# Transposing tokens on VectorE in 32x32 blocks instead of on TensorE, in a transformer block with routed experts

## The chip, the cores and the metric

The kernel runs on one core of a Trainium2 chip. The metric is the device time in microseconds, the median of several runs. All data is float32.

A core has five engines that each run their own list of instructions in order: TensorE (PE, matmuls; PEld is its loading of weights), VectorE (DVE), ScalarE (ACT), GpSimd (POOL) and SyncE (SP), which only issues transfers. Transfers run on 16 DMA engines. An engine that waits for a semaphore holds up everything behind it in its list.

## The reference

The input is x with 32 batches of 256 tokens of 128 features, 8192 tokens in all. Shift, scale and gate vectors for each batch come from a small product (`mod`). Then:

```python
h = _layernorm(x) * (1 + ca) + sa
x = x + ga * attn(h)        # 16 heads of 64; RMS norm of h first; softmax over the query axis
h = _layernorm(x) * (1 + cb) + sb
x = x + gb * moe(h)         # 32 experts in 4 groups: 2 groups a token, 6 experts among them,
                            # one anchor of 16, and a shared expert
```

What matters here is that products over features need the features of `h` on the partitions, while norms and rows in memory have a token on each partition. So each set of tokens is transposed, [tokens, features] to [features, tokens], at three places: ahead of attention, ahead of routing, and once more for each tile of tokens of the experts.

## The kernel before, in words

**Attention.** The tokens are cut into 16 chunks of 512 (`CH`), each as four blocks of 128 (`NT`). A step `s` is one pair of heads of one chunk, so there are 128 steps, eight for each chunk. The order is written out by hand (`manual_schedule`): a loop over `s` issues score products (`psc`, L438), the reduction of each row (`lowest`, L458, VectorE), exponentials (L468, ScalarE), the products with the values (`pav`, L505), query, key and value products of later steps (`pq` L402, `pk` L414, `pv` L388) and the projection (`po`, L526). Everything else that a chunk needs stands in `table`: a portion of work, the step relative to the chunk's first step, and the place in that step (TOP, MID or END). For instance

```python
(-8, END, norm1_scale),
(-5, END, norm1_turn),
...
(17, END, norm2_turn),
(18, END, route_logits),
```

mean that chunk c's first norm is finished at step 8c - 8 and turned at the end of step 8c - 5. `norm1_turn` and `norm2_turn` call `transposed`: four TensorE transposes (L326) into one PSUM bank, then a copy by ScalarE (L378, L571). `norm1_turn` makes `n_t`, the operand of the query, key and value products; `norm2_turn` makes `h2_all[c]`, the operand of `route_logits` and of the shared expert.

SP issues the transfers of this half: `load_x` and `load_mod1` at step -15 of a chunk, `load_mods` at step 7, and the 69 blanks. A blank writes 512 empty rows to `rows_d`, a buffer in device memory that takes the tokens sorted by expert group. A row there has 180 floats (720 bytes): the 128 features of a token, then 52 floats of routing weights and its place. GpSimd scatters each chunk's rows into it (`route_send`, L768).

**Shared expert and expert tiles.** After the steps a loop of seven rounds does the shared expert (`shared_up`, `shared_down`) beside the last portions of `table`. Then come 35 tiles (`LISTS`) of 512 rows of one group. Tile j has five rounds k (four pairs of experts and the anchors): `up` makes `pg` and `pu` (L1141, L1142), ScalarE the silu, VectorE two products (L1145 with `pu`, L1146 with the routing weights `bt`), and `down` sums into `py` (L1167). Work for later tiles is mixed in: `fetch_rows(j + 3)` and `fetch_weights(j + 2)` at k = 0, `weights_mine(j + 2)` at k = 1, `weights_turn(j + 2)` at k = 2, `rows_turn(j + 1)` at k = 3. `weights_turn` transposes the routing weights (L1109), writes them to device memory (`cd`, L1113) and, when that has landed, reads them back once for all partitions (`bt`, L1116, L1121). `rows_turn` transposes the rows' features by four TensorE transposes (L1132) and a copy by ScalarE (L1134).

`send(j)` scatters a tile's result to `y_d` (L1178). When all tiles of a chunk are surely done, `pass_load` (two loads `s`, L1234, and a gate, L1239) at k = 4, `pass_sum` at k = 1 of the next tile and `pass_out` (L1256) at k = 3 finish the chunk. With the levels of this kernel there is one `pass_load` in each of tiles 17 to 27, then in 29, 30, 33 and 34. All these transfers are issued by SP in program order.

## Time and profile before

| | us |
|---|---|
| median of 3 runs | 1537.22 (1533.1 to 1537.77) |
| profiled execution, its own time | 1516.82 |
| span of that execution, first to last instruction | 1515.0 |
| busy: TensorE, VectorE, ScalarE, GpSimd | 1447.8, 1019.8, 837.3, 775.2 |
| mean granted TensorE clock | 0.987 |
| first score product, first expert tile | 39.6, 986.3 |

Four transposes and one copy turn one chunk or tile. In the profile by forms they are:

| line | what | instructions | mean ns |
|---|---|---|---|
| L326 | `ptn`, TensorE | 64 | 299 |
| L326 | `pth`, TensorE | 64 | 289 |
| L1132 | `ph`, TensorE | 140 | 273 |
| L378, L571, L1134 | copies, ScalarE | 16, 16, 35 | 585 |

How to read it: matmuls overlap in TensorE's pipeline, so a mean of 273 to 299 ns is not what one of them adds to the time; the distance between the starts of what stands before and after is. The share of busy time says little where halves of the program have different limits, so the slices, the windows and the chain of waits are read by stage.

### The profile page before, as it was taken

The page shows a single profiled execution, that of the slowest core. Times are in us where ns is not written, and L with a number is a line of the kernel's source. Part 1 is how long each engine was busy: PE and PEld are TensorE (multiplying, and loading weights), DVE is VectorE, ACT ScalarE, POOL GpSimd, SP SyncE. Part 2 cuts the span into 40 slices and gives each one's busy share as a digit, 9 for nine tenths or more (in the row PEclk, how much of TensorE's full clock was granted, in tenths as well). Part 3 has the DMA queues.
Part 4 walks back from the last instruction along what each step waited for, and adds up shares of the span by engine and source line. Part 5 has one row for each costly group of instructions (what it writes and reads, how often), then busy time and mean ns, then how long its engine had stood idle before and what let it go on. Part 6 is the DMA issues. An engine that isn't in the chain of part 4 may idle for free. (4 is left out here: it accounts for less than half of the span.)

```text
span 1515.0 us, 29937 instructions
## 1 busy us (share of the span) xinstructions
PE 1447.8 (96%) x8784; PEld 920.3 (61%) x8784; DVE 1019.8 (67%) x4239; ACT 837.3 (55%) x2796; POOL 775.2 (51%) x1311
## 2 busy tenths in 40 slices
PE   3999999999999999999999999899999999999994
PEld 1566666666666666666666666566666666565662
DVE  2655677677677677787677676666755556666663
ACT  1877677677677677676776767433333333333331
POOL 5335457567566566576576554744322324333333
PEclk7999999999999999999999999999999999999997
DMA  6970001000100100100110000576676677888862
GB/s 226 379 267 23 8 28 37 28 27 29 41 30 27 41 29 28 39 32 27 39 32 25 23 23 28 145 201 185 185 182 188 188 195 229 244 227 236 221 179 67
DMA packets 100073, 166.27 MB, mean 110 GB/s; under 512 B 15365, under 2 KB 58853, under 8 KB 95433
## 3 DMA queue, kind: packets, MB, share of 16 engines
q1 hardware_dynamic: 87096, 141.47, 32.8%
q0 software_dynamic: 10624, 20.21, 3.8%
q10 hardware_dynamic: 2192, 2.68, 0.5%
q8 instruction: 73, 1.20, 0.3%
q14 instruction: 88, 0.71, 0.2%
HBM read 113.51 MB, written 51.58 MB: 109 GB/s over the span
## 5 line engine op out<-in xcount | busy, mean ns | idle before, releaser
L468 ACT ACTIVATE e<-e,mn 128x256 f32<-128x256 f32 (+1 forms) x1024 | 454.6, 445 | 211.0 <-DVE mn L458 210.3
L458 DVE CUSTOM_DVE_ANT_0 e<-psc,mask 128x256 f32<-128x256 f32 (+1 forms) x1024 | 306.1, 346 | 63.5 <-PE psc L438 62.4
L1178 POOL DMA_INDIRECT y_d<-y,iy x140 | 139.6, 997 | 301.0 <-ACT y L1175 268.7
L487 POOL TENSOR_TENSOR vs<-v,rc 128x256 f32<-128x256 f32 x256 | 151.2, 611 | 272.5 <-DVE rc L476 249.2
L1145 DVE TENSOR_TENSOR a<-a,pu 128x512 f32<-128x512 f32 x175 | 119.9, 685 | 158.8 <-PE pu L1142 158.6
L438 PE MATMUL psc<-q,k 64*128 64x256 f32 (+1 forms) x2048 | 202.1, 337 | 0.0
L505 PE MATMUL pav<-e,vs 128*64 128x256 f32 (+1 forms) x2048 | 195.3, 333 | 4.2 <-POOL vs L487 4.2
L1144 ACT ACTIVATE a<-pg 128x512 f32<-128x512 f32 x175 | 104.5, 597 | 170.0 <-PE pg L1141 167.7
L1167 PEld LDWEIGHTS py<-wd_sb,a 128*128 128x128 f32 x1120 | 145.6, 192 | 84.1 <-issue 43.9
L407 DVE TENSOR_SCALAR q<-pq,negbq 128x512 f32<-128x512 f32 x128 | 96.0, 750 | 148.1 <-PE pq L402 147.6
L468 ACT ACTIVATION_READ_ACCUMULATOR e<-e,mn 128x1 f32 x1024 | 191.6, 187 | 0.0
L438 PEld LDWEIGHTS psc<-q,k 64*128 64x128 f32 x2048 | 166.4, 187 | 28.2 <-issue 7.9
L1141 PE MATMUL pg<-h,wg 128*128 128x512 f32 x350 | 179.7, 595 | 0.0
L1142 PE MATMUL pu<-h,wu 128*128 128x512 f32 x350 | 178.8, 593 | 0.0
L526 PEld LDWEIGHTS po<-wo_sb,z 128*128 128x128 f32 x1024 | 134.9, 193 | 59.6 <-issue 59.6
L505 PEld LDWEIGHTS pav<-e,vs 128*64 128x64 f32 x2048 | 127.1, 137 | 56.7 <-POOL vs L487 4.5
L1167 PE MATMUL py<-wd_sb,a 128*128 x1120 | 149.4, 277 | 11.3 <-DVE a L1146 11.1
L768 POOL DMA_INDIRECT rows_d<-rows,ix x128 | 130.7, 1021 | 37.2 <-issue 34.2
L388 PE MATMUL pv<-wqkv_sb,n_t 128*128 128x512 f32 x256 | 145.4, 652 | 4.0 <-DVE q L407 3.2
L402 PE MATMUL pq<-n_t,wqkv_sb 128*128 128x512 f32 x256 | 144.1, 645 | 0.0
L526 PE MATMUL po<-wo_sb,z 128*128 128x128 f32 x1024 | 136.3, 277 | 0.0
L414 PE MATMUL pk<-n_t,wqkv_sb 128*128 128x512 f32 x256 | 130.8, 592 | 0.0
(214 smaller groups left out, 1851.2 us busy)
## 6 DMA issues: line engine op xcount, KB each, us to landing
bt<-cd SPq DMA_DIRECT2D x70, 512.0 KB
rows_d<-blank SPq DMA_DIRECT2D x69, 360.0 KB
rw<-rows_d SPq DMA_DIRECT2D x35, 360.0 KB
wg<-in_w_gate_dram SPq DMA_DIRECT2D x35, 256.0 KB
wu<-in_w_up_dram SPq DMA_DIRECT2D x35, 256.0 KB
bt<-cd SPq DMA_DIRECT2D x140, 64.0 KB
mb<-mod_dram SPq DMA_DIRECT2D x32, 256.0 KB
s<-y_d SPq DMA_DIRECT2D x32, 256.0 KB
```

The costliest lines, as they stand in the source:

```text
L388: nc.tensor.matmul(pv, chunk[c]["n"][:, i * P : (i + 1) * P], wqkv_sb[:, 2, j * CH : (j + 1) * CH], start=True, stop=True,)
L402: nc.tensor.matmul(pq, wqkv_sb[:, 0, t * P : (t + 1) * P], chunk[c]["n"], start=True, stop=True)
L438: nc.tensor.matmul(pb[h][:, cols], k[r, o + kb * P : o + (kb + 1) * P], q[r, o + kb * P : o + S], start=True, stop=True,)
L458: nc.vector.tensor_tensor_reduce(e[:, cols], ps[:, cols], mask[:, cols], 1.0, 3e38, ALU.add, ALU.min, mn[:, b, kb, h : h + 1],)
L468: nc.scalar.activation(e[:, cols], e[:, cols], AF.Exp, bias=mn[:, b, kb, h : h + 1], scale=-1.0, accum_out=sm[:, b, kb, h : h + 1],)
L487: nc.gpsimd.tensor_tensor(vs[:, 2 * b : 2 * b + 2], vt[:, 2 * b : 2 * b + 2, col : col + P].rearrange("p k (h d) -> p k h d", h=2), rc[:, ...
L505: nc.tensor.matmul(pav[h * DH : (h + 1) * DH, o + kb * P : o + S], vs[:, 2 * b + kb, h, :], e[:, 0 : 2 * P] if kb == 0 else e[:, 2 * P : 3 ...
L526: nc.tensor.matmul(chunk[c]["po"][:, i, :], z[:, i * P : (i + 1) * P], wo_sb[:, t, :], start=t == 0 and i == 0, stop=t == NP - 1 and i == ...
L1141: nc.tensor.matmul(pg, t["wg"][:, k, :], t["h"], start=True, stop=True)
L1142: nc.tensor.matmul(pu, t["wu"][:, k, :], t["h"], start=True, stop=True)
L1167: nc.tensor.matmul(t["py"][:, i, :], a[:, i * P : (i + 1) * P], w, start=k == 0 and i == 0, stop=k == KU and i == NT - 1,)
L1178: sent = nc.gpsimd.indirect_dma_start(out=y_d[:, :], out_offset=bass.IndirectOffsetOnAxis(ap=ix[:, i : i + 1], axis=0), in_=y[:, i, :], in ...
```

## The change

Three turns go from TensorE and ScalarE to VectorE, whose transpose works inside 32x32 blocks. So the blocks must be in place before: `load_blocks` reads the tokens from device memory with four transfers, one for each 32 features, that put piece c of every 32 tokens on partition 32b + c. In memory such a piece is 32 floats, 128 bytes, and a set of 512 tokens has 2048 of them.

- `norm1_turn` (but for chunk 0) and `norm2_turn`: a new portion, `norm1_send` at -7 END and `norm2_send` at 16 END, writes the tokens to a buffer in device memory (`hd`, two buffers) and reads them back by blocks (`through_dram`); the turn is one VectorE transpose. `norm1_turn` moves from -5 END to -5 MID, `norm2_turn` from 17 END to 19 TOP, `route_logits` from 18 to 19 END. The buffer `hb` has the tag of the normalized tokens (`xhln1`, `xhln2`), so it takes their place.
- Tiles: `fetch_rows` loads the 52 floats of routing (208 bytes a row) and the features apart, by four block loads; `rows_turn` is one VectorE transpose. The order of a tile's tokens goes from `(p i)` to `(i p)`.
- Blanks: three a step, after the portions at END, instead of five a step ahead of everything.

```diff
+        hdp = actx.enter_context(tc.tile_pool(name="hd", bufs=2, space=DRAM))
...
+        def load_blocks(dst, rows):
+            return [
+                nc.sync.dma_start(
+                    out=dst[b * BLK : (b + 1) * BLK],
+                    in_=rows[:, b * BLK : (b + 1) * BLK].rearrange("(x c) r -> c x r", c=BLK),
+                )
+                for b in range(P // BLK)
+            ]
+
+        def through_dram(src, tag, name):
+            hd = hdp.tile([CH, D], F32, tag="hd", name=f"hd_{name}")
+            nc.sync.dma_start(out=hd.rearrange("(i p) d -> p i d", p=P), in_=src)
+            hb = ln.tile([P, CH // BLK, BLK], F32, tag=tag, name=f"hb_{name}")
+            load_blocks(hb, hd)
+            return hb.rearrange("p x r -> p (x r)")
...
         def norm1_turn(c):
-            nc.scalar.copy(n_t, transposed(chunk[c].pop("h"), f"ptn_{c}"))
+            if c == 0:
+                nc.scalar.copy(n_t, transposed(chunk[c].pop("h"), f"ptn_{c}"))
+            else:
+                nc.vector.transpose(n_t, chunk[c].pop("hb"))
+        def norm1_send(c):
+            if c > 0:
+                chunk[c]["hb"] = through_dram(chunk[c].pop("h"), "xhln1", f"ln1_{c}")
...
         def norm2_turn(c):
-            nc.scalar.copy(h2_all[c], transposed(chunk[c]["rows"][:, :, 0:D], f"pth_{c}"))
+            nc.vector.transpose(h2_all[c], chunk[c].pop("hb2"))
+        def norm2_send(c):
+            chunk[c]["hb2"] = through_dram(chunk[c]["rows"][:, :, 0:D], "xhln2", f"ln2_{c}")
...
-            (-5, END, norm1_turn),
+            (-7, END, norm1_send),
+            (-5, MID, norm1_turn),
...
-            (17, END, norm2_turn),
-            (18, END, route_logits),
+            (16, END, norm2_send),
+            (19, TOP, norm2_turn),
+            (19, END, route_logits),
...
-            for i in blanks[s * 5 : s * 5 + 5]:
-                write_blank(i)
...
             deal(s, END)
+            for i in blanks[s * 3 : s * 3 + 3]:
+                write_blank(i)
...
-            t["rw"] = rwp.tile([P, NT, ROW], F32, tag="rw", name=f"rw_{j}")
-            got = nc.sync.dma_start(
-                out=t["rw"],
-                in_=rows_d[bass.ds(r, CH), :].rearrange("(p i) f -> p i f", i=NT),
-            )
+            t["rw"] = rwp.tile([P, NT, ROW - D], F32, tag="rw", name=f"rw_{j}")
+            t["rh"] = rwp.tile([P, CH // BLK, BLK], F32, tag="rh", name=f"rh_{j}")
+            rows = rows_d[bass.ds(r, CH), :]
+            got = [
+                nc.sync.dma_start(
+                    out=t["rw"], in_=rows[:, D:].rearrange("(i p) f -> p i f", p=P)
+                ),
+                *load_blocks(t["rh"], rows),
+            ]
...
         def rows_turn(j):
             t = T[j]
-            rw = t.pop("rw")
-            ph = ps_mm.tile([P, CH], F32, tag="mm", name=f"ph_{j}")
-            for i in range(NT):
-                nc.tensor.transpose(ph[:, i * P : (i + 1) * P], rw[:, i, 0:D], ident)
             t["h"] = mp.tile([P, CH], F32, tag="h", name=f"h_{j}", bufs=2)
-            nc.scalar.copy(t["h"], ph)
+            nc.vector.transpose(t["h"], t.pop("rh").rearrange("p x r -> p (x r)"))
```

More of the change, by code (lines that the diff above doesn't have):

```diff
@@ L28 @@
 BPC = CH // S
+BLK = 32
 NCH = B * S // CH
@@ L1063, in fetch_rows @@
             r = nc.sync.value_load(of.table[0:1, 1, n : n + 1], min_val=0, max_val=NG * SPAN)
-            t["rw"] = rwp.tile([P, NT, ROW], F32, tag="rw", name=f"rw_{j}")
-            got = nc.sync.dma_start(
-                out=t["rw"],
-                in_=rows_d[bass.ds(r, CH), :].rearrange("(p i) f -> p i f", i=NT),
-            )
-            if j < FIRST:
-                tc.declare_no_dep(
-                    got.ins, group="late rows", reason="this tile holds rows of earlier chunks"
-                )
-                tc.add_to_no_dep_group("first tiles", got.ins)
+            t["rw"] = rwp.tile([P, NT, ROW - D], F32, tag="rw", name=f"rw_{j}")
[7 more added lines that the diff above has]
+            ]
+            if j < FIRST:
+                for d in got:
+                    tc.declare_no_dep(
+                        d.ins, group="late rows", reason="this tile holds rows of earlier chunks"
+                    )
+                    tc.add_to_no_dep_group("first tiles", d.ins)
         def fetch_weights(j):
@@ L1093, in weights_mine @@
                 mm,
-                t["rw"][:, :, D:].rearrange("p i (g w) -> p i g w", w=GW),
+                t.pop("rw").rearrange("p i (g w) -> p i g w", w=GW),
                 of.mine[:, n, :].unsqueeze(1).unsqueeze(3).to_broadcast([P, NT, NG, GW]),
```

## The prediction

> **What bounds the kernel now.** I read the slices first. TensorE is full from start to end; the 16 DMA engines are nearly idle in the attention half and 50 to 80% busy in the expert half.

> ```profile
> PE   3999999999999999999999999899999999999994
> ...
> DMA  6970001000100100100110000576676677888862
> ```

> A full row could still hide waits, so I read TensorE's timeline over attention steps (a step begins with `psc`). The step from 398.87 holds four transposes of L326 and takes 7.43 us; the next holds none and takes 6.87. Matmuls follow each other without a gap: in attention TensorE is the bound, and four transposes there cost 0.55 us.

> ```profile
> 398.87 1.58 PE L438 MATMUL psc<-q,k 64*128 64x256 f32 x16
> ...
> 405.71 0.66 PE L326 MATMUL ptn<-ident,ln_xh 128*128 128x128 f32 x4
> 406.30 1.58 PE L438 MATMUL psc<-q,k 64*128 64x256 f32 x16
> ...
> 413.17 1.58 PE L438 MATMUL psc<-q,k 64*128 64x256 f32 x16
> ```

> Next the expert tiles. From the starts of `pg`, tiles 8 to 17 take 13.92 us each, but tiles 18 to 28 (1242.7 to 1409.1 us) 15.13 on average. The windows (sum in us of TensorE, its weight loads, VectorE, ScalarE, GpSimd, then clock, DMA share, GB/s) show why I treat them apart. The first holds tiles 9 to 12: TensorE is busy all the time. The second holds tiles 22 to 27: TensorE is busy 93%, DMA 85%.

> ```profile
> 1117.30:1173.00 55.70, 55.70 (x274) 36.26 (x274) 32.03 (x53) 18.92 (x32) 15.54 (x16) 1.00 0.72 191
> 1302.30:1393.60 91.30, 84.91 (x410) 53.84 (x409) 60.60 (x97) 28.38 (x48) 35.14 (x36) 1.00 0.85 234
> ```

> The chain of waits says what ends last there: it leaves TensorE and runs through the DMA queue, the weights written (`cd`), read back (`bt`), then the expert sums of `pass_load` (`s`), which VectorE waits for ahead of the products of the next tile.

> ```profile
> 1341.82 3.16 DMA cd<-cwt
> 1345.03 4.66 DMA bt<-cd
> 1349.71 5.24 DMA s<-y_d
> ...
> 1357.07 1.25 DVE a L1146
> ```

> SP's own waits give its slack. The first row is slack in the TensorE-paced tiles (SP there waits some 4 us a tile for `cwt`); the second is the landing it must sit out in every tile.

> ```profile
> SPq L1113 <- ACT cwt L1111: 92.0, 24, 6.7
> SPq L1116 <- DMA cd<-cwt: 67.2, 35, 4.6
> ```

> [...]L1246 here took 691. No transpose on VectorE is in the trace; I take 0.7 us.[...]

> **The change, part by part.**

> *TensorE.* L326 loses 15 of its 16 `ptn` groups and all 16 `pth`; L1132 loses all 35. Two `pth` groups (chunks 14, 15) lie after the full steps. 29 x 0.55 + 2 x 0.5 = 17 us in attention and its tail. In a tile the step with `ph` takes 3.05 us against 2.61: 0.44 each. In the 24 tiles that TensorE paces that is 10.5 us; in the 11 DMA-paced ones nothing. ScalarE's 66 copies (585 ns) go too; it is 55% busy and never last, so nothing.

> *VectorE.* 66 transposes of 0.7 us. In attention two fall in one step (19 TOP and -5 MID, both 3 modulo 8). Its timeline in such a step has 0.95 us idle ahead of `lowest`, 1.35 ahead of `q`, 0.38 ahead of `v`, 2.7 in all, against 1.4 added and 0.55 that the step shortens: covered. If a transpose took over 1.1 us, `q` and then `pv` would be late. In tiles VectorE idles 1.2 to 2.1 us ahead of each `a`: covered; without that cover it would be 35 x 0.7 = 25 us. Moving `route_logits` from 18 to 19 END takes the same 1 us of TensorE; `route_sigmoid` at 20 MID still comes a step later.

> *SP and DMA in attention.* Each chunk gains twice: a 256 KB write, a wait for its landing, four block loads. By `cd` (1.5 us for 24 KB) plus 512 packets of 27 ns over 16 engines (0.9) the write lands after 2.4; four issues of 0.45; then some 2.5 to land: 7 to 8 us. For `norm1_turn` the scaled rows are ready at 562.5 (chunk 10) and the transpose is due 0.9 step later than the loads land; for `norm2_turn` the slack is 1.8 steps. Behind the wait on SP stand `load_x` and `load_mod1` of the next chunk: x now lands about when `norm1_moments` wants it (569.5 against 570). I take nothing; lower end nothing; upper end 2 us late, which after VectorE's slack is 1.4 us on `pv`, 13 times, 18 us. Blanks at 3 a step, behind the sends, end by step 22; the first rows go out at step 27. TensorE had no gap under the blanks, so nothing either way.

> *Start of the experts.* SP does `norm2_send` 14 before the first three row fetches, which now issue 15 DMAs instead of 3 (12 x 0.55 = 6.6 us more), then weights, `cd`, `bt` for two tiles, and only then `norm2_send` 15. Its transpose stands in VectorE's order in tile 0 near 993 us; my reckoning of SP lands its blocks at 997 to 1001. TensorE absorbs 1 to 2 us. Cost 4 us, bounds 0 and 8.

> *Tiles.* `rw` was one DMA of 128 packets of 2880 bytes, 162 ns in the crowded window: 1.30 us of 16 engines. Now there are 512 packets of 208 bytes and 2048 of 128. The trace's packet records have 128-byte packets at 12.4 to 13.2 ns, 256-byte ones at 18.5 and 512-byte ones at 27.2 in the first window, 30.9 in the second. Scaled by that 1.14: (2048 x 14.5 + 512 x 18) / 16 = 2.4 us. Lower end, unscaled: 2.1. Upper end: no stretch of the trace starts small packets faster than 690 a us, so 2560 need 3.7.[...] D = 1.3 us more DMA a tile (0.8 to 2.4).
> In a TensorE-paced tile DMA is busy 10.0 us; 11.3 and the landing wait of 1.1 fit in 13.48. SP issues four DMAs more (2.2 us), within its 4 us. Covered, with some 2 us left on each. In a DMA-paced tile 12.9 us of DMA and 2.3 of bubble make up the 15.2; D comes on top. What is late next is `cd`, which waits behind the block loads in the queue, so `bt`, so `s`, so VectorE and `py`. Eleven tiles follow a pass load: 14.3 us, and 1.5 for the slack that no longer absorbs the first of them.

> *Sum.* -17 - 10.5 + 4 + 14.3 + 1.5 = -7.7 us. Against the profiled execution's 1516.8 us (span 1515.0, 1.8 us around it, which the change does not touch): 1509.1. The median of the runs shown, 1537.2, is 20.4 us above that execution; I carry the difference over: 1529.5, rounded to **1530 us**.

> **The rivals.**

> *The block loads are dear* (slower). Place: `load_blocks` in `fetch_rows`; price: D. The gains of 27.5 us less the 5.5 of the start and the lost slack are eaten at D = 2.0; from D = 2.4 (under 690 packets a us) the kernel is slower by over 0.3%, and from 2.3 (13.5 less 10.0 and the landing wait of 1.1) DMA also paces the other 24 tiles. At D = 2.8: 11 x 2.8 + 24 x 0.5 + 5.5 - 27.5 = +21, 1558 us. For: 85% DMA already, and a queue in which everything stands behind everything. Against: 32-byte packets took 9 ns, so packets as such are cheap.

> *The loads hide.* If the bubble of 2.3 us in DMA-paced tiles takes D in and the start costs nothing: -27.5, 1510 us. For: that bubble exists. Against: it stands between `cd` and `bt`, where SP issues nothing else.

> *Attention waits for its data.* `load_x` comes late and VectorE stops at `norm1_moments`: +18 on my sum, 1548 us; it decides from 0.6 us of lateness on, what VectorE's idle time does not take in. For: half a microsecond of slack. Against: VectorE idles 2.7 us in the step that follows.

> That the change does not do what it says, I exclude: SP's and TensorE's instruction order of the changed kernel has the loads and lacks the transposes.

> **How the numbers follow.** About 0.3% (4.6 us) is what a measurement can tell from no change. My forecast (D 0.8 to 1.8) has 0.50 and spans 1522 to 1539: faster 0.37, same 0.13. Dear loads 0.30, slower. Hiding 0.13, faster. Late attention 0.07, slower. Faster 0.50, same 0.13, slower 0.37. The forecast's own range is 1522 to 1539; with the other cases, 1511 to 1560.

> **What would show it.** Right: attention steps without transposes all at 6.9 us, 7.9 with `route_logits`; TensorE-paced tiles at 13.5; tiles 18 to 28 at 16 to 17, still with `cd`, `bt`, `s` in the chain; a VectorE wait for `hb` in tile 0; transposes near 0.7 us. Wrong: 128-byte packets over 20 ns or tiles 8 to 17 above 13.9 (dear loads); VectorE idle ahead of L290 or the transposes of attention (late data); tiles 18 to 28 at 15 or less (hidden).

## The result, and the profile after

The changed kernel takes 1551.2 us (median of 4 runs, 1549.8 to 1553.0), the kernel before 1535.9 beside it: ratio 1.0103, 95% interval 1.0085 to 1.0122. It is 15 us slower; the forecast was 1530 us (1522 to 1539), faster. The profiled execution of the changed kernel took 1549.8 us (span 1548.0).

One thing has to be known to read the numbers. The runs of this study came on several chips, and the kernel before takes 1533 to 1536 us on some and 1517 to 1518 us on others. The execution of it that the prediction was read from (1516.8) fits the second sort, the changed kernel's profile the first. A second profile of the kernel before, from a chip where it takes 1533 us (e1 below, span 1532.1), is therefore the right partner for the profile after. Ratios are always within one chip.

Two rows of the slices answer to those shown of before, and one is new: the TensorE clock that the throttle granted (`PEclk`), in tenths.

```profile
PE   3999999999999999999999998889999988888894
PEclk9999999999999999999999998999999999899997
DMA  4843621121121122122021113687888888788772
```

TensorE now shows eights in two places, the start of the experts and the tiles from 18 on, and the clock dips in the same slices. In attention TensorE's timeline shows what was forecast: from one `psc` to the next 7.87 us with `route_logits` (393.27 to 401.14), then 6.87 and 6.88, and no transposes.

```profile
393.27 1.58 PE L466 MATMUL psc<-q,k 64*128 64x256 f32 x16
...
401.14 1.58 PE L466 MATMUL psc<-q,k 64*128 64x256 f32 x16
...
408.01 1.58 PE L466 MATMUL psc<-q,k 64*128 64x256 f32 x16
...
414.89 1.36 PE L466 MATMUL psc<-q,k 64*128 64x256 f32 x12
```

The windows (columns as in the prediction) hold tiles 9 to 12, now 13.5 us each, and all of tiles 18 to 28:

```profile
1125.20:1179.20 54.00, 54.00 (x259) 34.54 (x259) 34.55 (x57) 16.16 (x28) 15.55 (x16) 1.00 0.87 195
1246.60:1440.90 194.30, 162.01 (x707) 101.41 (x706) 115.72 (x188) 44.98 (x77) 64.28 (x66) 0.91 0.82 206
```

The same tiles 18 to 28 of the kernel before, in its second profile, took 171.5 us:

```profile
1254.70:1426.20 171.50, 159.05 (x750) 100.27 (x750) 109.29 (x177) 50.84 (x88) 64.45 (x66) 0.98 0.82 225
```

So by stage, in us, worked out from the starts of `psc` and `pg` (tile 0 starts with its first `pg`):

| stage | before (e1) | after | difference |
|---|---|---|---|
| up to the last `psc` | 945.9 | 932.6 | -13.3 |
| last `psc` to tile 0 | 45.9 | 45.9 | 0 |
| tiles 0 to 7 | 123.7 | 133.2 | +9.6 |
| tiles 8 to 17 | 139.2 | 134.9 | -4.4 |
| tiles 18 to 28 | 171.5 | 194.3 | +22.8 |
| tile 29 to the end | 105.9 | 107.2 | +1.3 |

The sum is +16. On a chip of the other sort (e13 against the profile of 1516.8) the differences are -13.1, +3.2, +5.0, -4.4, +23.2 and +4.2, in all +18. The loss thus sits in two places. The sizes are good to some us only: between three profiles of the changed kernel (here, e9, e13) tiles 18 to 28 differ by up to 8 us, between the two of before by 5.

**Tiles 18 to 28.** The chain of waits ends in the last stores and no longer passes through these tiles, so I read SP's own timeline, one round of it (one tile's DMA issues), first of before:

```profile
1279.25 0.34 SPq L1065 DMA_DIRECT2D rw<-rows_d  x1
1279.84 0.34 SPq L1080 DMA_DIRECT2D wg<-in_w_gate_dram  x1
...
1281.90 0.37 SPq L1113 DMA_DIRECT2D cd<-cwt  x1
1285.56 1.10 SPq L1116 DMA_DIRECT2D bt<-cd  x2
...
1289.23 1.24 SPq L1234 DMA_DIRECT2D s<-y_d  x2
1292.55 0.32 SPq L1239 DMA_DIRECT2D gate<-gate_dram  x1
1294.42 0.34 SPq L1065 DMA_DIRECT2D rw<-rows_d  x1
```

and of after:

```profile
1290.60 0.40 SPq L1101 DMA_DIRECT2D rw<-rows_d  x1
1291.20 2.24 SPq L335 DMA_DIRECT2D rh<-rows_d  x4
1293.68 0.35 SPq L1118 DMA_DIRECT2D wg<-in_w_gate_dram  x1
...
1295.77 0.37 SPq L1151 DMA_DIRECT2D cd<-cwt  x1
1297.90 1.11 SPq L1154 DMA_DIRECT2D bt<-cd  x2
...
1301.57 1.58 SPq L1268 DMA_DIRECT2D s<-y_d  x2
1305.24 0.32 SPq L1273 DMA_DIRECT2D gate<-gate_dram  x1
1307.60 0.04 SPq L1101 DMA_DIRECT2D rw<-rows_d  x1
```

The round was 15.2 us and is 17.0. SP is never idle for long in it: it issues, sits out the landing of `cd` ahead of `bt`, and stops again ahead of `gate`, which the profile puts down to the landing of `bt`. Over all rounds between tiles 18 and 29 the mean was 15.9 us (e1) and is 17.2. What has grown is the time for issuing, not the waits for landings: from `rw` to the second `wg` issue (a tile's `wg` comes by two) SP takes 3.7 us on average (1.7 in e1), while its waits for the landing of `cd` over this stage, 26.3 us, lie between the 20.6 of e1 and the 31.4 of the first profile of before. That SP had no slack in these tiles stood in the first profile, in SP's waits of this stage alone (1243 to 1405 us; `cwt` are the routing weights that SP sends off as `cd`):

```profile
SPq L1116 <- DMA cd<-cwt: 31.4, 11, 3.4
...
SPq L1113 <- ACT cwt L1111: 1.7, 2, 1.0
```

Of the 92.0 us that SP waited for `cwt` over the whole kernel, 1.7 were here. SP also comes to these tiles late: from a tile's first `pg` to SP's row fetch in it there were 1.5 us in tile 8 and 1.4 in tile 17 (first profile of before); after the change there are 2.3 and 9.5. In tiles 9 to 16 SP's round is 14.0 us against TensorE's 13.49, and over the whole kernel its waits for `cwt` are down from 92.0 us to 7.5.

What follows the longer round is VectorE, which stands in order at `pass_sum` until `s` has landed, first e1 and then after (same stage):

```profile
DVE s L1246 <- DMA s<-y_d: 11.2, 7, 3.1
```

```profile
DVE s L1280 <- DMA s<-y_d: 32.3, 8, 6.7
```

While VectorE stands there, TensorE has no `a` for its `py`. In the timeline the 8 matmuls behind the longest of these stops take 2.08 us; the group before it took 1.05:

```profile
1321.67 1.05 PE L1201 MATMUL py<-wd_sb,a 128*128 x8
...
1331.52 2.08 PE L1201 MATMUL py<-wd_sb,a 128*128 x8 [6.64 <-DVE a L1180]
```

The granted clock was 0.50 there (1327.00 to 1337.30). By the two windows of tiles 18 to 28 above, 19.8 of the 22.8 us lost are idle time of TensorE (12.5 us before, 32.3 after). Its busy time grew by 3.0 us although 11 x 0.43 = 4.7 us of transposes went, so the slow matmuls took some 7.7 us more (an estimate). The tiles now come in pairs, a long one with a stop and slow matmuls and a short one that catches up, here tiles 21 and 22:

```profile
1301.20:1314.70 13.50, 13.50 (x66) 8.50 (x65) 10.10 (x18) 4.04 (x7) 5.88 (x6) 1.00 0.87 215
1314.70:1337.90 23.20, 16.56 (x66) 10.24 (x65) 10.91 (x19) 4.15 (x7) 5.77 (x6) 0.78 0.75 185
```

**The start of the experts.** VectorE stops in tile 0 for the blocks of chunk 15, as forecast, but for 6.51 us; TensorE stops 5.31 us and runs the next matmuls (`pl`, 1.92 us in place of 1.08) at a granted clock of 0.50 (994.20 to 996.20).

```profile
986.28 0.69 DVE L1180 TENSOR_TENSOR a<-a,bt 128x512 f32<-128x512 f32 x1
993.49 0.71 DVE L599 STREAM_TRANSPOSE h<-hb_ln 128x512 f32<-128x512 f32 x1 [6.51 <-DMA hb_ln<-hd_ln]
```

The cause is in SP's timeline: chunk 15's write and the block loads behind its landing, 5.8 us later. The write queues behind `bt` in the same queue: its packets of 512 bytes begin at 987 us, when those of `bt` are through.

```profile
983.57 0.39 SPq L345 DMA_DIRECT2D hd_ln<-rows  x1
989.35 1.91 SPq L335 DMA_DIRECT2D hb_ln<-hd_ln  x4
```

### The profile page after: what moved, and what is told of

Its sections match the earlier page's. It is cut to its first block, busy times and chain, and to the rows that moved or that the text cites. A ratio compares the mean times of both kernels' runs of the same rounds, so it can differ in the third digit from the quotient of the medians.

```text
span 1548.0 us, 30007 instructions
## 1 busy us (share of the span) xinstructions
PE 1435.8 (93%) x8520; PEld 902.5 (58%) x8520; DVE 1055.3 (68%) x4305; ACT 796.1 (51%) x2730; POOL 775.1 (50%) x1311
## 3 DMA queue, kind: packets, MB, share of 16 engines
q8 instruction: 70, 1.15, 0.3%
## 5 line engine op out<-in xcount | busy, mean ns | idle before, releaser
L1201 PEld LDWEIGHTS py<-wd_sb,a 128*128 128x128 f32 x1120 | 151.3, 198 | 118.8 <-DVE a L1180 61.4
L1201 PE MATMUL py<-wd_sb,a 128*128 x1120 | 155.9, 284 | 43.6 <-DVE a L1180 43.2
L1175 PE MATMUL pg<-h,wg 128*128 128x512 f32 x350 | 186.0, 614 | 0.0
L1176 PE MATMUL pu<-h,wu 128*128 128x512 f32 x350 | 182.2, 602 | 0.0
```

Of the source, the lines that this page charges most:

```text
L1175: nc.tensor.matmul(pg, t["wg"][:, k, :], t["h"], start=True, stop=True)
L1176: nc.tensor.matmul(pu, t["wu"][:, k, :], t["h"], start=True, stop=True)
L1201: nc.tensor.matmul(t["py"][:, i, :], a[:, i * P : (i + 1) * P], w, start=k == 0 and i == 0, stop=k == KU and i == NT - 1,)
```

## The experiments

Three theories for the tiles from 18 on. **SP issue time**: SP's round is a series of issues and landings, and four issues more make it 2 us longer. **DMA time**: the small pieces keep the DMA engines busier (the step on record). **Halved clock**: VectorE's waits make gaps in TensorE's work, and the halved clock that comes with them (0.50 in the stretch above) is what is lost.

### The kernel before again (e1)

No edit.

> The kernel before, run again, for a second profile of it: its only profiled execution took 1516.8 us, its timed ones 1533 to 1538. If the 20 us between them belong to how the expert tiles fall out, this profile shows some of its tiles 18 to 28 (15.1 us each in the first profile), or the shared stage, longer and the rest as before; if the profile of 1516.8 is simply a stray fast execution of every stage, all stages are longer. Time 1533 to 1538 us.

1533.3 us against 1533.1, ratio 1.0003 (0.9992 to 1.0013). Its profile (span 1532.1) is 17 us above the first one: +4.5 between attention and tile 0, +6.6 in tiles 0 to 7, +5.1 in tiles 18 to 28, 1.0 up to the last `psc`, nothing in tiles 8 to 17. It has two drops of the clock in tiles 18 to 28, where the first profile had none. So nearly all of what differs between these two profiles lies in the stages in which SP and DMA set the pace.

### Attention alone, tiles alone (e2, e3)

```
# e2: fetch_rows, rows_turn, weights_mine as before; norm1/norm2 through DRAM
# e3: fetch_rows, rows_turn, weights_mine as after; norm1/norm2 on TensorE, blanks 5 a step
```

> Only the attention half is changed: norm1 and norm2 go through DRAM and VectorE, the expert tiles load whole rows and turn them on TensorE as before. All theories: attention 12 us shorter, as in the changed kernel. Theory 'SP's issues set the pace of the heavy tiles'[...]: tiles 18 to 28 at 15.3 us as before. The start of the experts keeps the two sends of chunks 14 and 15 but only three row loads, not fifteen: 6 us of the changed kernel's 20 us loss there go. In all 1525 to 1533 us.

> Only the expert tiles are changed (four block loads and one load of weights a tile, turned by VectorE); attention is as before. Tiles 8 to 17 at 13.5 us (0.43 less each). Theory 'SP issue time': tiles 18 to 28 at 17.3 us, 2 us over before (four issues more, 0.55 us each, in SP's serial round), 22 to 27 in all; the first tiles lose less than in the changed kernel as no send of chunks 14 and 15 stands in SP's queue: +6 instead of +20. In all 1548 to 1556 us. Theory 'DMA time': tiles 18 to 28 at most 1.6 us over before each, in all 1540 to 1548.

e2: 1525.0 us, ratio 0.9934 (0.9907 to 0.9960). Attention ends 14.9 us earlier; tiles 0 to 7 take 2.6 us more than in e1, tiles 18 to 28 4.1 more, where nothing was expected (two profiles of one kernel differ by as much). e3: 1557.6 us, ratio 1.0166 (1.0139 to 1.0193), just above what 'SP issue time' said and far above 'DMA time'. Tiles 8 to 17 at 13.49 us, tiles 18 to 28 at 17.8 on average, 24.6 us over e1; tiles 0 to 7 only 1.8 us over e1. So the attention half is a gain and the tiles alone are a loss of 24 us; the loss in tiles 18 to 28 needs nothing from attention. The first tiles lose most only where both parts are there.

### The block loads on ScalarE's queue (e4)

```
-                nc.sync.dma_start(       # in load_blocks, for the tiles
+                nc.scalar.dma_start(
                 ...                     # ScalarE also reads the place of the rows for itself
```

> The changed kernel with the four block loads of each tile issued by ScalarE on its own queue in place of SP. Packets, bytes and buffers are the same. Theory 'SP issue time': SP's round in tiles 18 to 28 is 2.2 us shorter, so these tiles go back from 17.3 to about 15.1 us on average (22 us less), the start of the experts gains up to 6 us, in all 1522 to 1532 us, and the TensorE clock no longer falls in those tiles. Theory 'DMA time': the DMA work is the same, the tiles stay at 16.7 to 17.3, in all 1546 to 1552. Theory 'halved clock from VectorE waiting at the sums': the wait for s is shorter only as far as SP is earlier, in between.

1602.2 us, ratio 1.0466 (1.0414 to 1.0518), outside all three. The four issues cost ScalarE about what they had cost SP (2.87 us below, 2.24 in the round of after shown above), and ScalarE stands in TensorE's path: its `a` waits 3.12 us behind them.

```profile
1237.34 2.87 ACTq L335 DMA_DIRECT2D rh<-rows_d  x4
1240.31 1.08 ACT L1179 ACTIVATE a<-pg 128x512 f32<-128x512 f32 x2 [3.12 <-DMA rh<-rows_d]
```

Tiles 8 to 17 went from 13.5 to 15.7 us. For the theories this is inconclusive, since it added a new wait. It shows that ScalarE, though it is busy less than half of the time here, had no room for 2.9 us in one piece.

### Pieces and issues taken apart (e5, e6)

```
# e5: four issues, whole row parts: 512-byte pieces
-  in_=rows[:, b*32:(b+1)*32].rearrange("(x c) r -> c x r", c=32)
+  in_=rows[b*128:(b+1)*128, 0:D].rearrange("(c x) d -> c x d", c=32)
# e6: one issue, the same 2048 pieces of 128 bytes
-  *load_blocks(t["rh"], rows)
+  nc.sync.dma_start(out=t["rh"], in_=flat.rearrange("(p x s) -> p x s", x=16, s=45)[:, :, 0:32])
```

> The changed kernel, but each of a tile's four block loads brings 32 whole stretches of 2 KB in place of 512 pieces of 128 bytes: the same bytes from the same rows, the same four issues on SP, 128 packets a tile in place of 2048. The features land in the wrong places, so this times the traffic and not the result. Theory 'SP issue time': tiles 18 to 28 stay within 0.5 us of the changed kernel's 17.7 on average, in all 1545 to 1553 us. Theory 'DMA time of the small pieces': DMA work falls by 1.5 us a tile, tiles 18 to 28 go back to 15.5 to 16, in all 1530 to 1536.

> The changed kernel, but the four block loads of a tile are one DMA with the same 2048 pieces of 128 bytes, taken from the tile's rows at even distances of 180 bytes (the features land in the wrong places, so this times the traffic and not the result). Theory 'SP issue time': SP's round is 1.6 us shorter, tiles 18 to 28 at 15.7 to 16.2 on average, the start of the experts 3 to 6 us shorter, in all 1524 to 1534 us. Theory 'DMA time of the small pieces': nothing changes, 1547 to 1553.

Both ran on a chip where before takes 1516.9 us. In e5 the rows lie 720 bytes apart, so the pieces were of 512 bytes, 512 a tile, and not of 2 KB as the expectation says. e5: 1545.7 us, ratio 1.0185 (1.0168 to 1.0202). e6: 1517.4 us, ratio 1.0007 (1.0000 to 1.0015). The DMA engines' busy time per tile (from the packets, over tiles 18 to 28) was 13.4 us in e5 and 13.8 in e6, but the tiles took 18.4 and 16.3: the kernel with less DMA work is the slower one. In e5's window the DMA share falls to 0.73 while the tiles get longer:

```profile
1235.10:1437.00 201.90, 162.53 (x706) 101.44 (x705) 115.43 (x188) 45.62 (x77) 63.51 (x66) 0.92 0.73 198
```

Each of its four issues also took longer (0.62 us in place of 0.43 in e13), and SP's round was 18.1 us. That the DMA engines' work sets the length of these tiles falls here. The total of e5 lies in the range that 'SP issue time' gave, but that range was meant for the slower sort of chip: against the changed kernel on a chip of this sort (e13, 1534.7) e5 is 11 us slower, which neither theory said.

### Late sums, and the last two chunks on TensorE (e7, e8)

```
# e7
-                if k == 1 and summing:      pass_sum     -> k == 3
-                if k == 3 and summing:      pass_out     -> k == 4
# e8
+            if c >= NCH - 2:  norm2_turn by transposed(...), no norm2_send
```

> The changed kernel with VectorE's addition of the expert sums two steps later in a tile (k = 3) and the output one step later (k = 4), so that VectorE no longer stands before s has landed. Loads and DMAs are the same. Theory '[...]that is what the tiles lose': no drop of the clock in tiles 18 to 28, which take 16.3 or less on average, in all 1530 to 1538 us. Theories 'SP issue time' and 'DMA time': SP's round or the DMA work is as long as it was, the same time comes out as waiting elsewhere (weights or bt), tiles 18 to 28 stay at 17 to 17.7, in all 1545 to 1552.

> The changed kernel, but the normalized rows of chunks 14 and 15 are turned on TensorE as before, so that SP sends neither of them through DRAM at the start of the experts (two writes, two waits for landing, eight block loads fewer). Theory: the 6.5 us for which VectorE waits for the blocks of chunk 15 in tile 0 go, and with them most of that tile's 21.9 us: tile 0 at 13.5 to 15, the shared stage 3 us shorter, TensorE pays 1 us for the transposes; in all 1538 to 1543 us. Rival: the start is held by the queue behind the three row loads and the weights of two tiles anyway, and tile 1 or 2 takes the wait over: 1546 to 1551.

Same chip as e5 and e6. e7: ratio 1.0055 (1.0038 to 1.0072); without the changed kernel on that chip its effect stays open (e15 below). e8: ratio 1.0027 (1.0019 to 1.0035). There tile 0 takes 14.2 us and tiles 0 to 7 together 115.1, while e5 and e7, with the same start as the changed kernel, have 23.6 and 21.1 for tile 0 and 124.6 and 122.1 for the eight; the stretch ahead of tile 0 is 2.7 us shorter. So the wait for chunk 15's blocks, and with it 10 us or so of the start, is shown to come from the two late sends. They cost that only behind the added issues: e6, which has the sends but one issue in place of four, takes 14.3 us for tile 0 and 115.3 for the eight.

### Four bare issues on the kernel before (e9, e10)

```
+            rx = rwp.tile([1, 4, 32], ...)
+            for b in range(4):
+                nc.sync.dma_start(out=rx[:, b, :], in_=rows[b : b + 1, 0:32])
```

> The changed kernel run again beside the others of this call, as their partner on one chip: the kernel before took 1533 us on the chip of the first four runs and 1517 on that of the next four. Its ratio to the kernel before should be near the 1.010 measured at first; if the start of the experts is fast on this chip (tiles 0 to 7 in 117 us instead of 124 for the kernel before), 1.010 to 1.020.

> The kernel before with four DMAs more a tile on SP, of 128 bytes each, from the tile's rows into a tile that nothing reads. Theory 'SP issue time': SP's round in tiles 18 to 28 grows by 2 us (15.3 to 15.9 now), the tiles with it, 22 us in all; tiles 8 to 17 stay at 13.92, the start of the experts loses 0 to 5; ratio 1.013 to 1.018. Theory 'DMA time': four packets more a tile are nothing, ratio 0.998 to 1.002.

On one chip (before 1535.3): the changed kernel 1551.4, ratio 1.0096 (1.0069 to 1.0122); the kernel before with four more issues 1556.6, ratio 1.0132 (1.0111 to 1.0152). Four DMAs of 128 bytes a tile cost 21 us. In the profile SP's round between tiles 18 and 29 is 17.2 us, the `rx` issues stand where the `rh` loads stood, and the DMA share has gone down:

```profile
1299.92 0.34 SPq L1068 DMA_DIRECT2D rw<-rows_d  x1
1300.46 1.58 SPq L1070 DMA_DIRECT2D rx<-rows_d  x4
1302.31 0.36 SPq L1086 DMA_DIRECT2D wg<-in_w_gate_dram  x1
```

```profile
1258.90:1445.30 186.40, 164.91 (x750) 105.47 (x749) 109.48 (x177) 51.53 (x88) 64.18 (x66) 0.94 0.77 209
```

Tiles 18 to 28 took 186.4 us against e1's 171.5: of the 23 to 26 us that they lose in the changed kernel (after, e9), four issues that carry next to nothing make 15. The profiles come from two chips of the same sort, so this too is good to some us.

### Candidates (e11, e12)

```
# e11: e2 and e8 together; tiles as before.   e12: e11 with the sums of e7
```

> A candidate: attention's transposes on VectorE through DRAM as in the changed kernel, but those of norm2 of chunks 14 and 15, and those of all expert tiles, on TensorE as before. By the parts: attention 13 us shorter, the shared stage and the tiles as in the kernel before; ratio 0.990 to 0.993 (faster than both). If SP's sends in attention cost the experts something else, 0.994 to 1.0.

> The candidate before, with VectorE's sums of the experts at k = 3 of a tile and the output at k = 4. Theory 'VectorE waiting for s makes the gaps that halve the clock':[...] 2 to 6 us faster than the candidate. Theory 'SP issue time' alone: the same within 2 us, since SP's round does not change.

e11: 1521.0 us, ratio 0.9913 (0.9893 to 0.9933). e12: 1509.7 us, ratio 0.9834 (0.9818 to 0.9851): both beat both kernels. Late sums gained 11 us, more than either theory said; tiles 18 to 28 went from 172.8 to 162.9 us.

### The pairs on one chip (e13 to e16)

> The changed kernel as partner of the next three, on their chip. Ratio 1.007 to 1.012 where the kernel before takes 1533 to 1537 us, 1.010 to 1.020 where it takes 1517.

> The single issue for a tile's blocks (the same 2048 pieces of 128 bytes, features in the wrong places), beside the changed kernel on one chip. Theory 'SP issue time': 20 to 30 us below the changed kernel. Theory 'DMA time of the small pieces': within 3 us of it. Theory 'halved clock alone': within 10 us of it.

> Late sums on the changed kernel, beside it on one chip. Theory 'halved clock after VectorE's waits for s is what the tiles lose': 14 us or more below the changed kernel. Theory 'SP issue time, with the clock as an addition': 8 to 14 below, as late sums gained 11 us on the candidate. Theory 'SP issue time alone': within 4.

> Late sums on the kernel before. If VectorE's waits for s cost time there too (its second profile has two drops of the clock in tiles 18 to 28), 8 to 12 us faster than before, ratio 0.992 to 0.995; if these waits cost only the changed kernel, 0.998 to 1.002.

The edits are those of e6 and e7, and e7's on the kernel before. Before takes 1518.1 us there.

| kernel | us | ratio to before, 95% | tiles 18 to 28 |
|---|---|---|---|
| changed (e13) | 1534.7 | 1.0112 (1.0093 to 1.0130) | 189.6 |
| one issue (e14) | 1521.2 | 1.0027 (1.0019 to 1.0036) | 184.1 |
| late sums (e15) | 1533.1 | 1.0102 (1.0069 to 1.0134) | 185.0 |
| before, late sums (e16) | 1511.0 | 0.9956 (0.9941 to 0.9971) | 159.6 |

One issue in place of four takes 13.5 us off: less than 'SP issue time' said, far more than 'DMA time', and above the bound of 'halved clock alone'. By the profiles 6.5 us of it are in tiles 0 to 7 (SP reaches chunk 15's send earlier; VectorE waits 1.78 us for it instead of 5.00), 5.5 in tiles 18 to 28 and 3.7 in tiles 29 to 33. Tiles 18 to 28 remain 18 us above the 166.4 of the profile of 1516.8. That is not because SP's issues were gone and the DMA work was left: the one issue with 2048 pieces is not cheap for SP. In e14 the `wg` issue behind it takes 0.96 to 3.10 us in each of the eleven tiles (0.35 in e13); in six of them it also waits for TensorE, 6.0 us in all.

```profile
1302.15 0.62 SPq L1104 DMA_DIRECT2D rh<-rows_d  x1
1303.01 0.96 SPq L1123 DMA_DIRECT2D wg<-in_w_gate_dram  x1
1304.16 0.33 SPq L1127 DMA_DIRECT2D wg<-in_an_gate_dram  x1
```

Side by side, as means over tiles 18 to 28 in us:

| kernel | SP, from `rw` to the second `wg` | DMA engines busy, per tile | tile |
|---|---|---|---|
| before (first profile, e1) | 1.22, 1.67 | 12.7, 12.7 | 15.1, 15.6 |
| one issue (e6, e14) | 3.22, 3.27 | 13.8, 14.1 | 16.3, 16.7 |
| before, four bare issues (e10) | 3.65 | 13.0 | 16.9 |
| changed (after, e13, e9) | 3.71, 3.74, 3.96 | 14.4, 14.2, 14.3 | 17.7, 17.2, 18.0 |
| long pieces (e5) | 4.57 | 13.4 | 18.4 |

The tiles follow the time that SP spends on its issues and not the work of the DMA engines. Rows beside each other differ little more than two profiles of one kernel do (up to 0.8 us a tile), but two steps are clear: e10 lies 1.4 to 1.8 us above the kernel before with hardly more DMA work, and e5 1.6 to 2.1 us above the one-issue kernels with less of it. So it is SP's time that lengthens these tiles. Whether the small pieces cost something beyond it, as DMA work, stays open: from e10 to the changed kernel it is 0.3 to 1.0 us a tile, no more than such profiles differ by. Why the issue behind the 2048 pieces takes longer no run shows.

Late sums gain nothing measurable on the changed kernel (1.6 us between the medians, with runs from 1528 to 1538). But they didn't take the wait away: `s` lands so late that VectorE still stands for it, first e13 and then e15 over tiles 18 to 28:

```profile
DVE s L1280 <- DMA s<-y_d: 29.0, 10, 5.9
```

```profile
DVE s L1280 <- DMA s<-y_d: 23.1, 9, 4.5
```

The clock is halved for 27 us of these tiles in e15 and for 24 in e13 (mean granted clock 0.93 and 0.94). So e15 doesn't test what the halved clock costs the changed kernel; that stays open. As the only cause it is out, since most of the loss in tiles 18 to 28 is idle time of TensorE (19.8 of 22.8 us, above). On the kernel before late sums gain 7 us, a little less than forecast: tiles 18 to 22 run at 13.92 us in e16, and its clock does not fall in any of tiles 18 to 28. There SP came to these tiles on time, and in the changed kernel it is late by then. That this is why late sums do not help it is argued, not tested.

## Why the prediction was wrong

- **Attention, -17.** Right in its price: the steps without transposes take 6.88 us, with `route_logits` 7.87. Measured -13.3 up to the last `psc`, of which 1.5 is an earlier first `psc`. The rival "attention waits for its data" came true in two steps with `route_logits`: VectorE waits 3.09 and 1.46 us for x, and the steps from 164.14 and 793.50 take 9.8 and 8.8 us in place of 7.87.

```profile
165.78 0.87 DVE L292 BATCH_NORM_STATS2 ln_stats<-xt 128x6 f32<-128x128 f32 x4 [3.09 <-DMA xt<-in_x_dram]
```

- **VectorE, nothing.** Right: the transposes took 703 to 706 ns. The 0.7 us of the forecast was my assumption, with no transpose in the trace; L1246, a sum over as many elements (128x512), took 691 ns there. In attention and in TensorE's tiles the transposes lie beside TensorE's work (busy for 54.00 of 54.00 us in tiles 9 to 12).

```profile
L1168 DVE STREAM_TRANSPOSE h<-rh 128x512 f32<-128x512 f32 x35 | 24.6, 704 | 0.0
L599 DVE STREAM_TRANSPOSE h<-hb_ln 128x512 f32<-128x512 f32 x16 | 11.3, 703 | 8.1 <-DMA hb_ln<-hd_ln 8.1
```

- **TensorE-paced tiles, -10.5 over 24 tiles.** Right per tile (13.92 to 13.49) but only for tiles 8 to 17, -4.4. The 24 were too many from the start: in the first profile tiles 0 to 7 take 13.9 to 16.3 us.
- **Start of the experts, +4, bounds 0 and 8.** Mechanism right, size wrong. VectorE waits for the blocks of chunk 15 in tile 0, 6.5 us, inside the reckoning on record (wanted near 993, landed at 997 to 1001), and TensorE stops for 5.3 of them. But tile 0 lost 7.7 us, and tiles 0 to 7 together with the stretch ahead of them 9.6 us (8.2 on the other chip): the halved clock at the stop (0.50 for 6.8 us, from 992.55 on) was put at nothing.
- **D, 1.3 us a tile.** Near: the DMA engines were busy 12.7 us a tile before and 14.2 to 14.5 after; 128-byte packets took 14 ns, 208-byte ones 18. The 0.2 us in D above the scaled packet times (2.6 us in place of 2.4) was my assumption, which no trace had shown, and it doesn't show here: 14.5 ns was the reckoning without it. The rival "dear block loads" (D from 2.4 on, 1558 us) came near the time by luck, with a price that was not paid.
- **DMA-paced tiles, 14.3 + 1.5. This is the step that failed.** It measured +23. The working made these tiles longer by DMA time (D) alone and put SP's four issues at nothing: "SP issues four DMAs more (2.2 us), within its 4 us" was worked out for the tiles that TensorE paces and left out of the others. There SP had 1.7 us of `cwt` waits in 11 tiles, and its round of issues and landings was itself the pace; I took the bubble between `cd` and `bt` for DMA's only. The four issues stand in that round (e10: +15 in these tiles, with almost no DMA work).
- **SP's slack in the tiles ahead of them** was mis-sized too. In tiles 9 to 16 SP had 4.2 us of `cwt` waits a tile, but the stretch from `rw` to the second `wg` grew by 3.3 us (1.15 to 4.49) and a wait for the landing of `cd` by 1.0 (1.2 to 2.2). That used the slack up, and SP came to tile 18 some 7 us late. The first of the DMA-paced tiles takes 20.8 us against 14.2 in e1, where the prediction had 1.5 us for it.
- **The halved clock was not in the working at all.** The slow matmuls took some 7.7 us more in tiles 18 to 28 (estimate above). How much of that adds to SP's time, and how much lies beside it, is open.

The 20 us carried over between the execution that was read and the median were not a constant around the kernel: by e1's profile 16 of 17 us lie in the very stages that the change touches.

## What to carry to other kernels

A queue's slack is to be read stage by stage: a total of 92 us of waiting said nothing about the eleven tiles in which the queue had none. An issue took SP about half a microsecond here even where it carried 128 bytes (0.44 us from one to the next, e10), so splitting one load into five was paid in the queue's round even where the data was small (+15 us over tiles 18 to 28 in e10). Joining the pieces into one issue saved only part of it, since the issue behind the 2048 pieces took 0.96 to 3.10 us (e14) in place of 0.35 (e13). Count the issuing engine's time and the landings along the round before counting bytes. Keep a gain apart from its companion: here attention's transposes on VectorE were worth 9 parts in 1000 by themselves, once the last two chunks stayed on TensorE (e11), and moving a wait of VectorE later was worth 8 more on that kernel (e12), though nothing on the changed one (e15).
